# Forty columns of x a group on ScalarE from twenty packed words, and sixteen rows a group on the sync engine

## The chip, the cores and the metric

The kernel runs on one core of one Trainium2 chip. The metric is the device time of one launch in microseconds (us), the median of several runs. The engines named below are TensorE (PE, with PEld for its weight loads), VectorE (DVE), ScalarE (ACT), GpSimd (POOL) and the sync engine (SP); each runs its own list of instructions in order, and they meet through semaphores.

## The reference, cut to what matters

One layer of a graph network with attention over edges: 12500 nodes of 128 numbers, 212500 edges sorted by destination, 8 heads of 16 numbers.

```
Q, K, V = x @ WQ, x @ WK, x @ WV            # 12500 nodes, 8 heads of 16
Eh = edge_attr @ WE                         # 212500 edges
score = K[src] * Q[dst] / sqrt(16) * Eh
score = exp(clip(score.sum(-1), -5, 5))     # one number per edge and head
wV = segment_sum(V[src] * score, dst)
Z  = segment_sum(score, dst)
h  = x + wV / (Z + 1e-6)
y  = batchnorm over nodes(h) * gamma + beta
out = layernorm over features(x + y)
```

Everything is float32. The costly part is random access: each edge needs the K and V rows (256 numbers, 1 KB) of its source node.

## The kernel before, in words

The edges are cut into 1661 tiles of 128, in sorted order. A **group** is 8 tiles (the last has 5); there are 208 groups, numbered g from 0. The kernel first makes a table `kvd` in DRAM with the K and V row of every node, and keeps x, turned so that a node is a column of 128 numbers, in SBUF as `hx`. Then one loop over g (line 1004) does all edge work. In its iteration:

- DVE multiplies the gathered K rows of the group, which lie in a `slot`, by the edge projection and by the query in PSUM (`products`, L790: twice against `ps_e`, twice against `ps_q`), sums over a head (`scores`, L797), clips (L806); ACT takes the exponent (`clip_exp`, L807 and L808); DVE multiplies the V rows by it (`message`, L812).
- PE projects the next group's edge attributes (`eh_mm`, L765), spreads the queries to the edges (`qe_mm`, L774), and sums the messages by destination (`gather_sum`, L833).
- ACT takes the window of x for the queries (`q_window`, L719) and brings results out of PSUM (`q_out` L752, `sums_out` L838, `x_out` L875 and L876).

The K and V rows of a tile come into the slot in one of four ways. A tile is one of the 8 of its group, and only the last tile of a group (number 7) is ever fetched in another way than the first:

1. **A gather.** POOL issues one indirect DMA for the 128 rows of a tile (L290). Nine slots go round; when `message` of a group has been recorded, its slot is free and the gathers of a later group are queued (`load_kv`); `pace` ties each gather to a step of the iteration, so that they are spread over it.
2. **Columns on ACT** (`load_cols`, `fetch_cols`, L368 to L383). ACT loads node ids from `col_ids` into registers (L372) and copies, for each id, one column of `hx` into a tile `xc`, 128x1 an instruction (L383). In each group from 8 on it fetches COLS = 32: a load of 16 ids and 16 copies ahead of the exponent, a second load of 16 ids ahead of the exponent too, and 16 copies after it. When 128 columns are there, PE multiplies them by the K and V weights (`cols_mm`, L420) and ACT brings the 128 rows into the slot (`cols_out`, L425). The planner `col_plan` gives 49 groups whose last tile comes so.
3. **Rows on SP** (`fetch_rows`, L389 to L404). SP loads SP_ROWS = 8 ids a group from `row_ids` (L394) and issues one DMA of 1 KB for each, from `kvd` into a tile `byrow` (L401). When 128 rows are there, ACT copies the tile into the slot (`rows_out`, L411). `row_plan` gives 12 groups.
4. **Columns on DVE** (`fetch_v`, L364): 12 a group, 18 groups by `v_plan`.

So 49 + 12 + 18 = 79 groups need 7 gathers, not 8, and POOL issues 1518 gathers from `kvd`. Which group is served in which way follows from COLS, SP_ROWS and V_COLS alone; the ids of these tiles are put side by side on the host in that order.

SP's list also holds the loads of edge attributes (`load`, L700, 1 MB for two groups, ahead of the multiplication by two groups or more), the places of edges (`load_quad`, L588, once in four groups), and, about every ninth group, the write of 512 finished columns of h and the refill of their ring buffer (`keep_h`, L523 and L519). These wait for buffers that DVE, PE or ACT must have finished with.

An expression over registers, such as the address of a column from a node id, becomes one register instruction (FUSED_REGOPS in the trace) ahead of the copy that uses it.

Of the kernel before, what the change touches and what calls it, by code (L numbers as in the profile page):

```python
# [11 lines left out]
I32 = mybir.dt.int32  # L12
AF = mybir.ActivationFunctionType
OP = mybir.AluOpType
AX = mybir.AxisListType
ET = mybir.EngineType

P = 128
# [15 lines left out]
RING = 1024  # L34
MARGIN = 64
PAD = 2 * MARGIN + WN
COLS = 32
LOAD = 16
FIRST_COL = 8
COL_LAG = 3  # L40
SP_ROWS = 8
FIRST_ROW = 8
ROW_LAG = 2
NSEM = 6
# [31 lines left out]
def col_plan(sizes):  # L76
    full = sizes.count(U) // 2
    groups, end = [], P
    while FIRST_COL + -(-end // COLS) - 1 + COL_LAG < full:
        groups.append(max(NX, FIRST_COL + -(-end // COLS) - 1 + COL_LAG))  # L80
        end += P
    assert sorted(set(groups)) == groups
    return groups


def row_plan(sizes):
    full, used = sizes.count(U) // 2, set(col_plan(sizes))
    groups, end = [], P
    while True:
        g = FIRST_ROW + -(-end // SP_ROWS) + ROW_LAG  # L90
        while g in used:
            g += 1
        if g >= full:
            return groups
        used.add(g)
        groups.append(g)
        end += P


def v_plan(sizes):  # L100
    full, used = sizes.count(U) // 2, set(col_plan(sizes) + row_plan(sizes))
    tiles, at, end = [], [], P
    while True:
        m = FIRST_COL + -(-end // V_COLS)
        while (m - FIRST_COL) * COLS % P < COLS:
            m += 1
        g = m + COL_LAG - 1
        while g in used:
            g += 1
        if g >= full:  # L110
            return tiles, at
        used.add(g)
        tiles.append(g)
        at.append(m)
        end += P
# [7 lines left out]
def gnn_kernel(  # L123
# [19 lines left out]
    nc = tc.nc  # L143
    N, D = out.shape
# [10 lines left out]
    consts = ctx.enter_context(tc.tile_pool(name="consts", bufs=1))  # L155
# [53 lines left out]
    hx = consts.tile([P, N + P], F32, name="hx")  # L209
# [66 lines left out]
    def slot(i):  # L276
        return rows.tile([P, 2 * G * P], F32, name=f"slot{i}")

    first = slot(NSLOT).rearrange("p (h c d) -> p h c d", h=2, d=2 * P)
# [21 lines left out]
    def issue(n=0):  # L301
        while len(queued) > n:
            f, *a = queued.pop(0)
            f(*a)
# [11 lines left out]
    tot = len(col_tiles) * P  # L316
    assert -(-tot // (2 * COLS)) <= P and COLS == 2 * LOAD
    col_ids = consts.tile([P, 2 * COLS], I32, name="col_ids")
    row_tiles = row_plan(usizes)
    tot_rows = len(row_tiles) * P  # L320
    assert tot_rows % (2 * SP_ROWS) == 0 and row_tiles == sorted(row_tiles)
    v_tiles, v_at = v_plan(usizes)
# [4 lines left out]
    XV = {}  # L327
    row_ids = consts.tile([P, 2 * SP_ROWS], I32, name="row_ids")
    nc.vector.memset(row_ids, 0)
# [3 lines left out]
    XC = {}  # L333
# [3 lines left out]
    def load_ids(to, n, first, total):  # L337
        m, rest = divmod(total, n)
        for p, k, w in ((0, m, n), (m, 1, rest)):
            if w and k:  # L340
                nc.sync.dma_start(to[p:p + k, :w], bass.AP(
                    tensor=rsrc.tensor, offset=rsrc.offset + first + n * p, ap=[[n, k], [1, w]]))

    def load_col_ids():
        load_ids(col_ids, 2 * COLS, 0, tot)
        load_ids(row_ids, 2 * SP_ROWS, tot, tot_rows)
        load_ids(v_ids, 2 * V_COLS, tot + tot_rows, tot_v)
# [17 lines left out]

    OFFS = {}

    def load_cols(g, half):  # L368
        q = g - FIRST_COL
        if 0 <= q < -(-tot // COLS):  # L370
            at = q % 2 * COLS + half * LOAD
            _, offs = nc.values_load_multi_w_load_instructions(  # L372
                col_ids[q // 2:q // 2 + 1, at:at + LOAD], engines=(ET.Activation,), min_val=0, max_val=N - 1,
                skip_runtime_bounds_check_because="node ids")
            OFFS[g, half] = offs

    def fetch_cols(g, half):
        first = (g - FIRST_COL) * COLS + half * LOAD
        for r, off in zip(range(first, tot), OFFS.get((g, half), ())):
            k = col_tiles[r // P]  # L380
            if r % P == 0:
                XC[k] = late[0].tile([P, P], F32, name="xc", bufs=2)
            nc.scalar.activation(XC[k][:, r % P:r % P + 1], hx[:, ds(off, 1)], AF.Copy)  # L383

    def col_tile(g):
        q = (g - FIRST_COL) * COLS
# [2 lines left out]
    def fetch_rows(g):  # L389
        q = g - FIRST_ROW  # L390
        if not 0 <= q < tot_rows // SP_ROWS:
            return
        c = q % 2 * SP_ROWS
        _, offs = nc.values_load_multi_w_load_instructions(  # L394
            row_ids[q // 2:q // 2 + 1, c:c + SP_ROWS], engines=(ET.SP,), min_val=0,
            max_val=(N - 1) * 8 * P, skip_runtime_bounds_check_because="node ids")
        for r, off in enumerate(offs, q * SP_ROWS):
            k = r // P
            if r % P == 0:
                BY_ROW[k] = late[0].tile([P, 2 * P], F32, name="byrow", bufs=2)  # L400
            d = nc.sync.dma_start(BY_ROW[k][r % P:r % P + 1, :].bitcast(U8), kvb[ds(off, 8 * P)].unsqueeze(0))  # L401
            d.then_inc(rows_in[k % NSEM], 16)
            tc.no_tile_sem_insts.add(d.ins.name)
            tc.add_to_no_dep_group(f"rows{k}", d.ins)  # L404
# [78 lines left out]
    def within(f, g):  # L483
        return f(g) if 0 <= g < NG else None
# [100 lines left out]
    def load_quad(q):  # L585
        t = late[0].tile([P, RQ, U * P], U8, name="rbq", bufs=2)
        for h in (0, 1):
            nc.sync.dma_start(t[h * WN:(h + 1) * WN].rearrange("p a b -> p (a b)"), places(h, RQ * q, RQ))  # L588
        for k in range(RQ):
            RB[RQ * q + k] = t[:, k, :]  # L590
# [337 lines left out]
    for q in range(NQ):  # L928
# [13 lines left out]
        k = q - first_step  # L942
# [56 lines left out]
    def share(g):  # L999
        denom(g)  # L1000
        recip(g)
        attn(g)

    for g in range(NG - 2):
        within(load_rel, g + 3)
        if (g + 6) % RQ == 0 and (g + 6) // RQ in quads:
            load_quad((g + 6) // RQ)
        fetch_rows(g)
        if g % 2:
            load((g - 1) // 2 + 2)  # L1010
        within(products, g)
        within(scores, g)
        load_v(g)
        load_cols(g, 0)
        fetch_cols(g, 0)
        load_cols(g, 1)
        within(clip_exp, g)
        within(turned_onehot, g + 2)
        if g >= 2:
            share(g - 2)  # L1020
        late_x = g + 1 < nxg and g + 1 not in SLOT
        if late_x:
            turn_x(g + 1, 0, True)
            turn_x(g + 1, 4, True)
            project_main(g + 1)
        within(eh_mm, g + 1)
        within(qe_mm, g + 1)
        cols_mm(g)
        paced = g >= LATE + 4
        if not paced:  # L1030
            issue()
        else:
            issue(G)
            for step in (SENT[g - 1], PARTS[g][1], BY["eh", g + 1], PARTS[g][3], PARTS[g][4], BY["qe", g + 1]):
                pace(step)
        within(onehot, g + 1)
        if paced:
            pace(BY["one", g + 1])
        within(message, g)
        fetch_cols(g, 1)  # L1040
        within(q_window, g + 4)
        cols_out(g)
        rows_out(g)
        fetch_v(g)
        within(add_x, g - 3)
        within(q_mm, g + 3)
        within(gather_sum, g - 1)
        if paced:
            pace(BY["sum", g - 1])
        within(x_out, g - 3)  # L1050
        within(q_out, g + 3)
        within(sums_out, g - 1)
        if g == 2:
            load_last()
            nc.vector.tensor_scalar(row_ids, row_ids, 8 * P, None, op0=OP.mult)
        if g % (RUN // 2) == 2 and g > 2 and (g // (RUN // 2) + 1) * SEC < T:
            load_section(g // (RUN // 2) + 1)
        for i, r in enumerate(runs):
            if i and g == placed[i]:
                place(r)  # L1060
        within_checks(g)
        while free and todo and todo[0] in done and not pending:
            load_x()
        bn_parts(2 * g - 7, 2 * g - 5)
        if g == NG - 4:
            assert done >= set(range(NPRE))
            norm_first()
        if g == LATE - 1:
            tps.close()
            late.append(tps.enter_context(tc.tile_pool(name="late", bufs=1)))  # L1070
        if g == LATE - 2:
            free.append(NSLOT)
            load_kv()
    last = NG - 1
    g = last - 1
# [3 lines left out]
                           skip_runtime_bounds_check_because="a count")]  # L1079
# [332 lines left out]
```

## Time and profile before

| | |
|---|---|
| time, median of 3 runs | 2052.56 us (2050.99 to 2053.51) |
| the profiled execution | 2056.0 us, span of its instructions 2054.1 us |
| busy share of the span | PE 78%, PEld 63%, DVE 80%, ACT 51%, POOL 75% |
| mean granted TensorE clock | 0.874 |
| gathers from `kvd` on POOL | 1518, mean 952 ns |
| column copies on ACT | 6272, mean 190 ns |
| row DMAs on SP | 1536 |
| DMA queues' share of 16 engines | 33.2% (POOL's gathers), 24.2% (SP's) |

Busy time leaves out register, branch and semaphore instructions and the issue of DMAs, so SP has no busy share at all and ACT's does not hold its register loads. The idle time before an instruction is given with what ended it; "issue" there means that the engine waited for nothing that the profile shows. An engine that is idle in every step may still be the one that sets the pace, if its instructions follow each other at a fixed distance.

### The profile page before, as it was taken

To read this page: it belongs to the slowest core of one execution; us is meant where nothing else is said; L and a number is where in the kernel's file an instruction comes from. 1 tells how busy PE (TensorE), PEld (TensorE's weight loads), DVE (VectorE), ACT (ScalarE), POOL (GpSimd) and SP (SyncE) were. 2 spreads that over 40 slices of the span, in tenths; PEclk is the share of its full clock that TensorE was granted. 3 is DMA by queue.
4 is the path that set the end of the run, shared out by engine and by line. 5 is a ranking of instruction groups with operands and counts; after the bars stand their busy time and mean duration, and the time that the engine had idled before them with its cause. 6 is when DMAs were issued, how large, how long until landed. Compare 5 with 4: busy or idle time off the path is not lost.

```text
span 2054.1 us, 58951 instructions
## 1 busy us (share of the span) xinstructions
PE 1612.4 (78%) x12867; PEld 1300.0 (63%) x12867; DVE 1645.6 (80%) x5263; ACT 1046.3 (51%) x8290; POOL 1535.1 (75%) x1618
## 2 busy tenths in 40 slices
PE   7889888878777787777787877887877777777777
PEld 6777666666555665665566665666666666655666
DVE  4468999998887788788787887877877787877787
ACT  2245656664554555455455455454555555555436
POOL 7677777777777777777777777777777777777775
PEclk9899989998898888888888889888888898888899
DMA  7856655665555555555555556555555555555573
GB/s 262 294 174 186 205 184 174 200 203 168 172 184 176 173 184 168 175 183 168 181 182 178 170 170 190 179 162 186 184 159 187 183 158 185 165 178 184 170 245 128
DMA packets 130284, 377.69 MB, mean 184 GB/s; under 512 B 36112, under 2 KB 47547, under 8 KB 116091
## 3 DMA queue, kind: packets, MB, share of 16 engines
q0 software_dynamic: 74912, 203.26, 33.2%
q1 hardware_dynamic: 51816, 169.43, 24.2%
q14 instruction: 267, 2.18, 0.3%
q8 instruction: 103, 1.69, 0.3%
q10 hardware_dynamic: 3186, 1.13, 0.2%
HBM read 348.25 MB, written 25.44 MB: 182 GB/s over the span
## 4 chain that ended last, share of the span: by engine, by line
DVE 27%; DMA 25%; PE 20%; issue 19%; POOL 5%; ACT 2%; DVEq 2%; ACTq 0%; SPq 0%; POOLq 0%
DMA slot<-kvd,srcs 23%; DVE slot L790 9%; DVE s L797 8%; PE ps_q L774 5%; POOL slot L290 5%; PE ps_e L765 4%; PE ps_a L833 3%; DVE xv L364 2%; DVE ot L738 2%; PE ps_a L858 1%; DVEq L364 1%; DVE msg L812 1%; PE ps_e L900 1%; DVE s L806 1%; PE ps_q L900 1%
## 5 line engine op out<-in xcount | busy, mean ns | idle before, releaser
L290 POOL DMA_INDIRECT slot<-kvd,srcs x1518 | 1445.7, 952 | 467.0 <-issue 282.3
L383 ACT ACTIVATE xc<-hx 128x1 f32 x6272 | 647.0, 190 | 176.8 <-issue 142.6
L765 PE MATMUL ps_e<-w_e,ea 128*128 128x128 f32 x3322 | 496.7, 301 | 215.7 <-DVE slot L790 206.2
L765 PEld LDWEIGHTS ps_e<-w_e,ea 128*128 128x128 f32 x3322 | 431.6, 205 | 281.5 <-DVE slot L790 238.2
L774 PE MATMUL ps_q<-qs,ot 64*128 64x128 f32 x3322 | 374.3, 338 | 166.8 <-DVE slot L790 153.8
L790 DVE TENSOR_TENSOR slot<-slot,ps_e 128x512 f32<-128x512 f32 x410 | 273.2, 679 | 239.2 <-DMA slot<-kvd,srcs 202.0
L774 PEld LDWEIGHTS ps_q<-qs,ot 64*128 64x128 f32 x3322 | 303.5, 230 | 228.2 <-DVE slot L790 211.4
L833 PE MATMUL ps_a<-msg,oh 128*64 128x136 f32 x3322 | 316.5, 316 | 1.9 <-DVE msg L812 1.7
L807 ACT ACTIVATE ps_m<-s 128x64 f32<-128x64 f32 (+1 forms) x209 | 47.6, 228 | 500.6 <-DVE s L806 471.2
L797 DVE TENSOR_REDUCE s<-slot 128x64 f32<-128x1024 f32 (+1 forms) x208 | 249.9, 1202 | 19.4 <-DVE slot L790 0.9
L790 DVE TENSOR_TENSOR slot<-slot,ps_q 128x512 f32<-128x512 f32 x410 | 261.5, 678 | 1.0 <-PE ps_q L774 0.7
L833 PEld LDWEIGHTS ps_a<-msg,oh 128*64 128x64 f32 x3322 | 202.9, 150 | 88.4 <-issue 68.4
L812 DVE TENSOR_TENSOR msg<-slot,ps_m 128x1024 f32<-128x1024 f32 (+2 forms) x209 | 247.8, 1187 | 2.1 <-ACT ps_m L807 1.3
L876 ACT ACTIVATE ring<-ps_a 128x64 f32 x408 | 90.7, 222 | 155.1 <-PE ps_a L833 139.1
L364 DVE COPY xv<-hx 128x1 f32 x2304 | 155.8, 143 | 0.0
L731 DVE TENSOR_TENSOR oh<-ps_i,rel 128x512 f32<-128x512 f32 x208 | 141.7, 681 | 0.0
L858 PE MATMUL ps_a<-ident,at 128*128 128x128 f32 x408 | 112.5, 365 | 0.9 <-ACT os L838 0.9
L719 ACT ACTIVATE xw<-hx 128x64 f32 x416 | 82.4, 245 | 41.7 <-issue 23.6
L858 PEld LDWEIGHTS ps_a<-ident,at 128*128 128x128 f32 x408 | 81.6, 231 | 28.9 <-issue 5.6
L748 PE MATMUL ps_a<-w_q,xw 128*128 128x128 f32 x416 | 96.8, 321 | 0.4 <-ACT qs L752 0.4
L859 PE MATMUL ps_a<-xw,ident 128*128 128x128 f32 x408 | 95.8, 324 | 0.0
L738 DVE TENSOR_SCALAR ot<-rbq,wiota 128x512 f32<-128x512 uint8 x188 | 95.3, 507 | 0.0
(187 smaller groups left out, 1471.7 us busy)
## 6 DMA issues: line engine op xcount, KB each, us to landing
ea<-eaT SPq DMA_DIRECT2D x103, 1024.0 KB
byrow<-kvd SPq DMA_DIRECT2D x1536, 1.0 KB
slot<-kvd,srcs POOLq DMA_INDIRECT x1518
rbq<-relT SPq DMA_DIRECT2D x94, 128.0 KB
kvd<-slot SPq DMA_DIRECT2D x12, 512.0 KB
kvd<-t SPq DMA_DIRECT2D x12, 512.0 KB
ring<-xT SPq DMA_DIRECT2D x24, 256.0 KB
hT<-ring SPq DMA_DIRECT2D x23, 256.0 KB
```

What stands on the lines that cost most here:

```text
L290: return nc.gpsimd.indirect_dma_start(out=out, out_offset=None, in_=table, in_offset=bass.IndirectOffsetOnAxis(ap=part(SRC, e, 1), axis=0))
L364: nc.vector.tensor_copy(XV[k][:, r % P:r % P + 1], hx[:, ds(off, 1)])
L383: nc.scalar.activation(XC[k][:, r % P:r % P + 1], hx[:, ds(off, 1)], AF.Copy)
L731: by(("one", g), nc.vector.tensor_tensor(one, iota_ps[:, None, :WN].to_broadcast([P, k, WN]), r[:, :, None].to_broadcast([P, k, WN]), op=O ...
L738: by(("ot", g), nc.vector.tensor_scalar(OT[g], RB[g], wiota, None, op0=OP.is_equal))
L765: by(("eh", g), nc.tensor.matmul(t[:, j - a, :], EA[g][:, j, :], w_e, start=True, stop=True))
L774: by(("qe", g), nc.tensor.matmul(QE[g][h][:, j, :], OT[g][r, j * P:(j + 1) * P], QS[g][r], start=True, stop=True))
L790: step = nc.vector.tensor_tensor(kv, kv, of[g][i][:, :b - a, :], op=OP.mult)
L797: step = nc.vector.tensor_reduce(SS[g][:, a:b, :], KV[g](a, b, 0).rearrange("p t (h d) -> p t h d", d=DH), axis=AX.X, op=OP.add)
L812: step = nc.vector.tensor_tensor(MSG[g][:, a:b, :P].rearrange("p t (h d) -> p t h d", d=DH), KV[g](a, b, P).rearrange("p t (h d) -> p t h ...
L833: by(("sum", g), nc.tensor.matmul(AGG[g][h * WN:(h + 1) * WN], OH[g][h * n + j], MSG[g][:, h * n + j, :], start=(j == 0), stop=(j == k - 1)))
L858: nc.tensor.matmul(ps, AT[g], ident, start=True, stop=False)
```

## The change

COLS goes from 32 to 40 and LOAD from 16 to 20; SP_ROWS goes from 8 to 16. Once, in iteration 2, DVE packs the node ids two to a 32-bit word (`pack_ids`: the odd one shifted left by 16, or-ed with the even one; an id is below 12500). `load_cols` becomes one load of 20 words a group; the two ids of a word are `w % 65536` and `w >> 16`, register expressions in front of the copy that uses them. The 40 copies stand as 20 ahead of the exponent and 20 after `message`. The planners are as before and give 61 groups by columns on ACT, 24 by rows on SP and 18 by columns on DVE: 103 groups with 7 gathers, 1494 gathers in all.

```diff
-COLS = 32
-LOAD = 16
+COLS = 40
+LOAD = 20
...
-SP_ROWS = 8
+SP_ROWS = 16
...
+    col_pairs = consts.tile([P, COLS], I32, name="col_pairs")
+    assert N < 1 << 15 and LOAD % 2 == 0
...
-    def load_cols(g, half):
+    def pack_ids():
+        two = col_ids.rearrange("p (n c) -> p n c", c=2)
+        nc.vector.scalar_tensor_tensor(col_pairs, two[:, :, 1], 16, two[:, :, 0], op0=OP.logical_shift_left,
+                                       op1=OP.bitwise_or)
+
+    def load_cols(g):
         q = g - FIRST_COL
         if 0 <= q < -(-tot // COLS):
-            at = q % 2 * COLS + half * LOAD
-            _, offs = nc.values_load_multi_w_load_instructions(
-                col_ids[q // 2:q // 2 + 1, at:at + LOAD], engines=(ET.Activation,), min_val=0, max_val=N - 1,
-                skip_runtime_bounds_check_because="node ids")
-            OFFS[g, half] = offs
+            at = q % 2 * COLS // 2
+            _, words = nc.values_load_multi_w_load_instructions(
+                col_pairs[q // 2:q // 2 + 1, at:at + COLS // 2], engines=(ET.Activation,), min_val=0,
+                max_val=(N << 16) - 1, skip_runtime_bounds_check_because="node ids")
+            OFFS[g] = [e for w in words for e in (w % (1 << 16), w >> 16)]
+
+    def column(at):
+        return hx[:, ds(nc.s_assert_within(at, 0, N - 1, skip_runtime_bounds_check_because="node ids"), 1)]
 
     def fetch_cols(g, half):
         first = (g - FIRST_COL) * COLS + half * LOAD
-        for r, off in zip(range(first, tot), OFFS.get((g, half), ())):
+        for r, at in zip(range(first, tot), OFFS.get(g, ())[half * LOAD:half * LOAD + LOAD]):
...
-            nc.scalar.activation(XC[k][:, r % P:r % P + 1], hx[:, ds(off, 1)], AF.Copy)
+            nc.scalar.activation(XC[k][:, r % P:r % P + 1], column(at), AF.Copy)
...
-        load_cols(g, 0)
+        load_cols(g)
         fetch_cols(g, 0)
-        load_cols(g, 1)
...
         if g == 2:
             load_last()
             nc.vector.tensor_scalar(row_ids, row_ids, 8 * P, None, op0=OP.mult)
+            pack_ids()
```

The line numbers of the changed kernel are 2 higher around the id tiles and 10 higher after the functions above (ACT's column copy is L393, the row DMA L411, the exponent L817).

On POOL, the gathers of groups 14 to 21, one row a group, before:

```order
L290 DMA slot_1108<-kvd,srcs 128x256 x7
L290 DMA slot_1334<-kvd,srcs 128x256 x8
L290 DMA slot_1399<-kvd,srcs 128x256 x8
L290 DMA slot_1669<-kvd,srcs 128x256 x8
L290 DMA slot_1916<-kvd,srcs 128x256 x7
L290 DMA slot_2162<-kvd,srcs 128x256 x8
L290 DMA slot_2408<-kvd,srcs 128x256 x8
L290 DMA slot_2654<-kvd,srcs 128x256 x7
```

and in the changed kernel:

```order
L290 DMA slot_1111<-kvd,srcs 128x256 x7
L290 DMA slot_1337<-kvd,srcs 128x256 x8
L290 DMA slot_1402<-kvd,srcs 128x256 x8
L290 DMA slot_1675<-kvd,srcs 128x256 x7
L290 DMA slot_1928<-kvd,srcs 128x256 x7
L290 DMA slot_2181<-kvd,srcs 128x256 x8
L290 DMA slot_2435<-kvd,srcs 128x256 x7
L290 DMA slot_2687<-kvd,srcs 128x256 x7
```

Five of these eight groups have 7 gathers where three had; over the program it is 24 gathers fewer, and nothing else moves on POOL.

On ACT, the place around the exponent of one group in the middle of the loop (the ISA rows are the register instructions that make a column's address), before:

```order
L383 ISA
L383 ACTIVATE xc<-hx 128x1
L372 TENSOR_LOAD col_ids
L807 ACTIVATE ps_m<-s 128x64
L808 ACTIVATE msg<-s 128x8x8
L383 ISA
L383 ACTIVATE xc<-hx 128x1
```

and in the changed kernel:

```order
L393 ISA
L393 ACTIVATE xc<-hx 128x1
L817 ACTIVATE ps_m<-s 128x64
L818 ACTIVATE msg<-s 128x8x8
L393 ISA
L393 ACTIVATE xc<-hx 128x1
```

The load between the copies and the exponent is gone, and one load of 20 words stands ahead of the first copy; there is still one register instruction for each copy, which now holds three operations (remainder or quotient, multiply, add) where it held two (multiply, add).

On SP, two groups in the middle of the loop, before:

```order
L700 DMA ea<-eaT 128x2048
L588 DMA rbq<-relT 64x2048 x2
L394 TENSOR_LOAD row_ids
L401 DMA byrow<-kvd 1x1024 x8
L394 TENSOR_LOAD row_ids
L401 DMA byrow<-kvd 1x1024 x8
L700 DMA ea<-eaT 128x2048
```

and in the changed kernel:

```order
L710 DMA ea<-eaT 128x2048
L598 DMA rbq<-relT 64x2048 x2
L404 TENSOR_LOAD row_ids
L411 DMA byrow<-kvd 1x1024 x16
L404 TENSOR_LOAD row_ids
L411 DMA byrow<-kvd 1x1024 x16
L710 DMA ea<-eaT 128x2048
```

Sixteen row DMAs stand where eight did, so a load of edge attributes is issued behind 32 row DMAs since the one before it, not behind 16.

## The prediction

> **What bounds the kernel now.** I read the table of engines first: DVE 80%, PE 78%, POOL 75%, ACT 51%, none full. So the question goes to the waits, and there I began with the engine that never rests, POOL, by its timeline: here the first two gathers from `kvd` and the last two, with start, duration, and in brackets the idle time before.
>
> ```profile
> 90.95 0.94 POOL L290 DMA_INDIRECT slot<-kvd,srcs  x1 [4.69 <-issue]
> 92.20 0.95 POOL L290 DMA_INDIRECT slot<-kvd,srcs  x1 [0.30 <-issue]
> ...
> 1996.76 0.95 POOL L290 DMA_INDIRECT slot<-kvd,srcs  x1 [0.30 <-issue]
> 1998.01 0.95 POOL L290 DMA_INDIRECT slot<-kvd,srcs  x1 [0.30 <-issue]
> ```
>
> 1518 gathers lie between 90.95 and 1998.01, so they follow each other every 1907.06 / 1517 = 1.257 us, and the two ends show the plain spacing: 0.95 busy and 0.30 between, 1.25. Nearly nothing is left for waiting. The waits of POOL, DVE and ACT from 820 to 1990 us (total, times, longest) and the number of groups DVE did there say the same:
>
> ```profile
> POOL slot L290 <- issue: 164.5, 540, 0.3
> ...
> DVE slot L790 <- DMA slot<-kvd,srcs: 152.9, 91, 5.4
> ...
> L797 DVE TENSOR_REDUCE s<-slot 128x64 f32<-128x1024 f32 x123 | 150.0, 1220 | 11.3
> ...
> ACT ps_m L807 <- DVE s L806: 293.3, 106, 7.1
> ACT ring L876 <- PE ps_a L833: 84.6, 46, 3.5
> ACT ring L875 <- PE ps_a L833: 25.3, 14, 2.8
> ```
>
> POOL's longest wait is the 0.3 us that stands before every gather; no step, slot or transfer holds it up. DVE waits for gathers to land. A group takes 1170 / 123 = 9.51 us, of which DVE waits 152.9 / 123 = 1.24 for gathers; left alone it would need about 8.27. POOL needs 1518 / 200 x 1.257 = 9.54 a group (groups 8 to 207). So **the issue of gathers on POOL** sets the loop's end, DVE is second with 1.2 us of room, and ACT waits (293.3 + 84.6 + 25.3) / 123 = 3.28 us a group for others.
>
> **The change, part by part.**
>
> *Gathers removed.* 1518 become 1494: 24 x 1.257 = **30.2 us** off a chain without gaps. POOL then needs 1494 / 200 x 1.257 = 9.39 us a group, still 1.1 above DVE's own 8.27, so all of it should arrive at the end. After the last gather nothing is changed, and the 56 us from there to the span's end stay. All 24 saved gathers belong to groups before the last few, so none is saved too late.
>
> *ACT: loads, copies, register work.* Rows of single lines (shortest, median, longest ns), and two runs of 16 copies:
>
> ```profile
> L383 ACTq FUSED_REGOPS  x6272: 37/37/37, 169.7 to 1974.5; - x196
> L875 ACTq FUSED_REGOPS  x83: 51/51/57, 250.8 to 1999.7; - x83
> L372 ACTq TENSOR_LOAD <-col_ids x392: 1007/1048/1461, 168.6 to 1969.4; - x196
> L866 ACTq TENSOR_LOAD <-ring_i x104: 306/312/488, 125.4 to 2008.0; - x104
> ...
> 1003.24 1.67 ACT L383 ACTIVATE xc<-hx 128x1 f32 x16 [0.62 <-issue]
> ...
> 1008.57 0.23 ACT L807 ACTIVATE ps_m<-s 128x64 f32<-128x64 f32 x1 [3.67 <-DVE s L806]
> 1008.73 0.24 ACT L808 ACTIVATE msg<-s 128x64 f32<-128x64 f32 x1
> 1008.88 1.57 ACT L383 ACTIVATE xc<-hx 128x1 f32 x16
> ```
>
> A load of 16 words takes 1.048, one of 4 words 0.312: 0.061 a word, so 20 words take 1.048 + 4 x 0.061 = 1.29. Two loads (2.10) become that one: -0.81 a group. Sixteen copies take 1.67 or 1.57, so one every (1.67 - 0.19) / 15 = 0.099 or 0.092, say 0.097; eight more are +0.78. Together -0.03: the packing pays for the columns. What is left is the added register operation of all 40 copies. The remainder and the quotient are in no row. Below, it costs nothing, if it falls into the spacing of the copies. The nearest row is L875, which adds one more term to an address than L383 does: 51 against 37 ns, 14 an operation. Above, I take the dearest work per register that the trace has, 61 ns a loaded word. A group then grows by 0, 0.56 or 2.45 us; I take 0.56, since that is the same instruction with one operation more. Even 2.45 lies within ACT's 3.28 (3.16 at the new pace). Ahead of the exponent stand one load and 20 copies, 1.29 + 20 x 0.111 = 3.5 us, where two loads and 16 copies took 3.65: the exponent is no later, and it waited 3.67 for DVE in the row above. Behind `message` the copies grow from 16 x 0.097 to 20 x 0.111, by 0.67; queued behind them are the window of x, `cols_out`, `rows_out`, `x_out` and `sums_out`. Those who wait for these are DVE and PE, and DVE's 1.24 us covers it; without that cover it would be 0.67 x 200 = 134 us. The 12 more `cols_out` and 12 more `rows_out` (0.38 and 0.41 each) are 10 us in all on ACT, 0.05 a group.
>
> *SP: sixteen rows.* SP's queue over eight groups, and its load:
>
> ```profile
> 999.67 1.10 SPq L588 DMA_DIRECT2D rbq<-relT  x2
> 1001.91 5.94 SPq L401 DMA_DIRECT2D byrow<-kvd  x16
> 1007.97 0.36 SPq L700 DMA_DIRECT2D ea<-eaT  x1
> 1009.22 6.72 SPq L401 DMA_DIRECT2D byrow<-kvd  x16
> 1025.02 0.36 SPq L700 DMA_DIRECT2D ea<-eaT  x1
> 1038.73 1.10 SPq L588 DMA_DIRECT2D rbq<-relT  x2
> 1040.98 5.96 SPq L401 DMA_DIRECT2D byrow<-kvd  x16
> 1047.03 0.36 SPq L700 DMA_DIRECT2D ea<-eaT  x1
> 1062.62 0.35 SPq L523 DMA_DIRECT2D hT<-ring  x1
> 1064.98 0.33 SPq L519 DMA_DIRECT2D ring<-xT  x1
> 1066.22 6.12 SPq L401 DMA_DIRECT2D byrow<-kvd  x16
> 1072.45 0.36 SPq L700 DMA_DIRECT2D ea<-eaT  x1
> 1075.23 1.09 SPq L588 DMA_DIRECT2D rbq<-relT  x2
> 1077.45 2.55 SPq L401 DMA_DIRECT2D byrow<-kvd  x8
> ...
> L394 SPq TENSOR_LOAD <-row_ids x192: 712/799/1001, 164.7 to 1909.7; - x192
> L401 SPq DMA_DIRECT2D byrow<-kvd x1536: 224/228/512, 166.6 to 1912.9; - x192
> ```
>
> Eight rows take 2.55, one every (2.55 - 0.23) / 7 = 0.33. Eight more are 2.65, and eight more words to load 8 x 0.061 = 0.49: +3.1 us a group, 25 us over these eight groups. SP's three long idle stretches there (1015.94 to 1025.02, 1025.38 to 1038.73, 1047.39 to 1062.62) are 9.1 + 13.4 + 15.2 = 37.7. So SP has room, but uses two thirds of it. A group's SP work becomes 16 x 0.33 + 1.29 + 0.18 (half of a load of edge attributes) + 0.28 (a quarter of `rbq`) + 0.3 (ring) = 7.3 us of 9.39.
>
> What gets late is what stands behind the rows. The edge attributes of two groups (1.05 MB) are asked for as soon as their buffer is free, two groups or 19 us ahead of use; behind four more groups' worth of eight rows they go out some 6 to 12 us later than now. The transfer itself I estimate from the window's rate:
>
> ```profile
> 820.00:1990.00 1170.00, 906.17 (x7193) 723.12 (x7193) 939.32 (x3078) 596.54 (x4949) 886.01 (x933) 0.85 0.57 180
> ```
>
> 1.05 MB at 180 GB/s (the last number) is 5.8 us, so 19 - 5.8 = 13 us are spare: enough, but no longer ample. The rows themselves have two groups (ROW_LAG) to land.
>
> [...]
>
> *PE and DVE.* Twelve more `cols_mm` fall on PE, which waits for DVE anyway; `pack_ids` is one small instruction of DVE in iteration 2, before the loop is short of anything. Both nothing.
>
> **Sum.** The profiled execution took 2056.0 (span 2054.1): 2056.0 - 30.2 = 2025.8. It lies 3.4 above the median of the runs, so for the median **2022.5**.
>
> **Rivals.**
>
> *A. ACT's remainders and quotients make it slower.* A remainder and a quotient are worked out for each of 20 words, in some 196 groups. ACT's room is 3.16 us a group; 40 of them fill it at 79 ns each, and at 83 ns the kernel is as slow as before (0.15 us x 200 groups = the 30 us won). At 100 ns it is 0.84 x 196 = 165 us over the forecast: about **2188**. For it: no row has such an operation, and it stands twice in every group, with the exponent behind one half. Against: one more operation costs 14 ns in L875, and a multiply is already among the two in L383.
> [...]
>
> *B. The edge attributes come late.* If SP's lateness eats the 13 us and PE waits w us for each load, DVE's pace becomes 8.27 + w / 2. That is nothing until w = 2.2; at w = 2.4 a group takes 9.47, 0.08 x 200 = 16 us more: about **2039**. For it: SP falls behind whenever a ring refill has held it for 15 us. Against: the idle stretches above let it catch up.
>
> *C. SP cannot keep up.* Its work passes 9.39 us when a row costs (9.39 - 2.05) / 16 = 0.46. At 0.51, the longest single issue in the row of L401, it is 10.2 a group, 0.8 x 192 = 155 us: about **2178**. Against: the median is 0.228 for the issue and 0.33 for the spacing.
>
> *D. The gain is lost in the start.* Early on DVE is behind POOL, and saved gathers could make POOL wait for slots. Then only the later ones count, and the time nears **2050**. Against: POOL's 0.30 us before a gather stays the same from 92 us on.
>
> **How the numbers follow.** The forecast, POOL's chain shorter by 24 gathers, has 0.80; its own range is 2017 to 2030 (the whole 30 us and a few us of noise, or a quarter of it lost at stalls). B has 0.06, A 0.07, C 0.03, D 0.04. The range 2017 to 2042 takes in the forecast and most of B. A measurement tells 0.2%, about 4 us, from no change: faster 0.80 + 0.05 from B = 0.85; same 0.05 from D and the end of B; slower 0.10 from A and C.
>
> **What would show it.** Right: 1494 gathers still every 1.25 to 1.26 us with 0.30 before them, the last near 1968; DVE's waits for gathers a little shorter (1.1 us a group); ACT's register instruction near 51 ns and its wait for DVE before the exponent near 2 us. Wrong: gaps before gathers (D), register instructions of 80 ns or more and DVE waiting for the exponent (A), PE waiting for `ea` (B), SP's queue without idle stretches (C).

## The result

The changed kernel takes 2021.17 us (median of 4 runs, 2019.15 to 2024.75) beside 2051.77 for the kernel before: 30.6 us less, ratio 0.985 with a 95% interval of 0.9836 to 0.9865. The prediction said 2022.5, between 2017 and 2042. The profiled execution took 2024.75 us, with a span of 2022.9. Nine of the twelve experiments below ran on two other chips, on which the kernel before itself takes 2620 or 2650 us, so each is compared with the kernel before on its own chip only, and what those two chips can tell is said apart.

### The profile after

POOL's timeline in the changed kernel: the first two gathers from `kvd` and the last two.

```profile
90.00 0.94 POOL L290 DMA_INDIRECT slot<-kvd,srcs  x1 [4.80 <-issue]
91.25 0.95 POOL L290 DMA_INDIRECT slot<-kvd,srcs  x1 [0.30 <-issue]
...
1964.80 0.95 POOL L290 DMA_INDIRECT slot<-kvd,srcs  x1 [0.30 <-issue]
1966.05 0.95 POOL L290 DMA_INDIRECT slot<-kvd,srcs  x1 [0.30 <-DVE slot L800]
```

1494 gathers in 1876.05 us are 1876.05 / 1493 = 1.2566 us each: the same spacing, 24 fewer. The last one starts 31.96 us earlier than before (1998.01 to 1966.05). The chain began 0.95 earlier, 24 x 1.257 = 30.2 are the gathers, and the last 0.8 are the mean spacing, which is shorter by a little over 0.0005 us at each of 1493 gathers. What follows the last gather took 56.1 us and now takes 56.9, so the span is 31.2 shorter.

The waits of DVE, PE and ACT (total, times, longest) from 820 to 1960 us, and the 122 groups that DVE did there:

```profile
DVE slot L800 <- DMA slot<-kvd,srcs: 125.0, 67, 5.1
DVE stats L889 <- ACT ring L886: 23.7, 14, 3.1
DVE msg L822 <- ACT ps_m L817: 9.0, 18, 1.0
...
L807 DVE TENSOR_REDUCE s<-slot 128x64 f32<-128x1024 f32 x122 | 148.8, 1220 | 10.8
...
PE ps_e L775 <- ACT slot L435: 28.6, 13, 3.3
PE ps_e L775 <- DMA ea<-eaT: 0.6, 1, 0.6
...
ACT ps_m L817 <- DVE s L816: 58.2, 38, 5.0
ACT ring L886 <- PE ps_a L843: 21.8, 25, 2.3
ACT ring L885 <- PE ps_a L843: 4.9, 7, 1.2
```

DVE still waits 125.0 / 122 = 1.02 us a group for gathers (1.24 before), so POOL is still the bound. The edge attributes come in time. What changed most is ACT: its waits, (58.2 + 21.8 + 4.9) / 122 = 0.70 us a group, were 3.28 in the same three rows (what of that was room is worked out below), and DVE and PE have begun to wait for it. Two lines and the timeline of one group say why; the columns of the first are the shortest, median and longest time in ns.

```profile
L393 ACTq FUSED_REGOPS  x7808: 73/77/100, 168.1 to 1940.1; - x196
L379 ACTq TENSOR_LOAD <-col_pairs x196: 1238/1296/2062, 166.7 to 1937.6; - x196
...
1001.86 2.83 ACT L393 ACTIVATE xc<-hx 128x1 f32 x20 [0.91 <-issue]
1004.60 0.21 ACT L817 ACTIVATE ps_m<-s 128x64 f32<-128x64 f32 x1
1004.74 0.24 ACT L818 ACTIVATE msg<-s 128x64 f32<-128x64 f32 x1
1004.89 1.78 ACT L393 ACTIVATE xc<-hx 128x1 f32 x14
```

The load of 20 words takes 1.296, as reckoned (1.29). The register instruction takes 77 ns, not 51: a remainder or a quotient of a word took 40 ns more here than the instruction without it (37, L383 before), where an added term took 14 (51, L885). Twenty copies take 2.83, one every (2.83 - 0.19) / 19 = 0.139 us; before it was 0.097. In this group ACT comes out of its 20 copies just as the exponent is due, without a wait.

SP's queue, the first seven of its entries from 999 to 1080 us, and its two lines:

```profile
999.78 0.36 SPq L710 DMA_DIRECT2D ea<-eaT  x1
1001.51 11.99 SPq L411 DMA_DIRECT2D byrow<-kvd  x32
1013.62 0.36 SPq L710 DMA_DIRECT2D ea<-eaT  x1
1023.35 1.11 SPq L598 DMA_DIRECT2D rbq<-relT  x2
1026.05 11.93 SPq L411 DMA_DIRECT2D byrow<-kvd  x32
1038.07 0.36 SPq L710 DMA_DIRECT2D ea<-eaT  x1
1044.26 0.35 SPq L533 DMA_DIRECT2D hT<-ring  x1
...
L404 SPq TENSOR_LOAD <-row_ids x192: 1158/1258/1489, 162.8 to 1887.5; - x192
L411 SPq DMA_DIRECT2D byrow<-kvd x3072: 224/228/415, 164.7 to 1893.7; - x192
```

Thirty-two rows and the load between them take 12 us, so a row still goes out every 0.33 us and a load of 16 ids takes 1.26. The long idle stretches shrank to 1013.98 to 1023.35 and 1038.43 to 1044.26, 15 us where 38 were; the prediction's 37.7 less 25 left 13. From there to 1080 us SP is never idle for longer than 3.1 us.

### The profile page after: what moved, and what is told of

Read it like the earlier page. It is cut to its first block, busy times and chain, and to the rows that moved or that the text cites. A ratio compares the mean times of both kernels' runs of the same rounds, so it can differ in the third digit from the quotient of the medians.

```text
span 2022.9 us, 65020 instructions
## 1 busy us (share of the span) xinstructions
PE 1609.2 (80%) x12891; PEld 1308.4 (65%) x12891; DVE 1648.2 (81%) x5264; ACT 1467.7 (73%) x9850; POOL 1511.8 (75%) x1594
## 4 chain that ended last, share of the span: by engine, by line
issue 22%; DMA 19%; DVE 19%; PE 16%; ACT 15%; POOL 4%; ACTq 2%; DVEq 1%; SPq 1%; POOLq 0%
DMA slot<-kvd,srcs 17%; ACT xc L393 10%; DVE slot L800 7%; DVE s L807 5%; POOL slot L290 4%; PE ps_q L784 4%; PE ps_e L775 3%; PE ps_a L843 2%; DVE xv L366 2%; ACT ring L886 2%; DVE ot L748 1%; PE ps_e L487 1%; PE ps_q L910 1%; PE ps_e L910 1%; DVEq L366 1%
## 5 line engine op out<-in xcount | busy, mean ns | idle before, releaser
L290 POOL DMA_INDIRECT slot<-kvd,srcs x1494 | 1421.9, 952 | 459.9 <-issue 283.4
L393 ACT ACTIVATE xc<-hx 128x1 f32 x7808 | 1073.3, 201 | 248.2 <-issue 215.5
L775 PE MATMUL ps_e<-w_e,ea 128*128 128x128 f32 x3322 | 524.7, 313 | 269.7 <-DVE slot L800 209.1
L775 PEld LDWEIGHTS ps_e<-w_e,ea 128*128 128x128 f32 x3322 | 458.3, 216 | 335.3 <-DVE slot L800 243.5
L784 PE MATMUL ps_q<-qs,ot 64*128 64x128 f32 x3322 | 358.0, 340 | 84.6 <-DVE slot L800 74.2
L784 PEld LDWEIGHTS ps_q<-qs,ot 64*128 64x128 f32 x3322 | 294.6, 234 | 138.2 <-DVE slot L800 121.0
L800 DVE TENSOR_TENSOR slot<-slot,ps_e 128x512 f32<-128x512 f32 x410 | 268.1, 679 | 141.5 <-DMA slot<-kvd,srcs 125.0
L843 PE MATMUL ps_a<-msg,oh 128*64 128x136 f32 x3322 | 305.1, 307 | 1.7 <-DVE msg L822 1.7
L843 PEld LDWEIGHTS ps_a<-msg,oh 128*64 128x64 f32 x3322 | 194.5, 145 | 83.9 <-issue 61.6
L868 PE MATMUL ps_a<-ident,at 128*128 128x128 f32 x408 | 107.0, 350 | 1.2 <-ACT os L848 1.2
L817 ACT ACTIVATE ps_m<-s 128x64 f32<-128x64 f32 (+1 forms) x209 | 45.0, 215 | 76.6 <-DVE s L816 75.2
L758 PE MATMUL ps_a<-w_q,xw 128*128 128x128 f32 x416 | 91.7, 307 | 0.4 <-ACT qs L762 0.4
```

Of the source, the lines that this page charges most:

```text
L290: return nc.gpsimd.indirect_dma_start(out=out, out_offset=None, in_=table, in_offset=bass.IndirectOffsetOnAxis(ap=part(SRC, e, 1), axis=0))
L393: nc.scalar.activation(XC[k][:, r % P:r % P + 1], column(at), AF.Copy)
L775: by(("eh", g), nc.tensor.matmul(t[:, j - a, :], EA[g][:, j, :], w_e, start=True, stop=True))
L784: by(("qe", g), nc.tensor.matmul(QE[g][h][:, j, :], OT[g][r, j * P:(j + 1) * P], QS[g][r], start=True, stop=True))
L800: step = nc.vector.tensor_tensor(kv, kv, of[g][i][:, :b - a, :], op=OP.mult)
L843: by(("sum", g), nc.tensor.matmul(AGG[g][h * WN:(h + 1) * WN], OH[g][h * n + j], MSG[g][:, h * n + j, :], start=(j == 0), stop=(j == k - 1)))
```

## Experiments

### Where the kernel before takes its 2052 to 2054 us

The theory to test was that the time follows the number of gathers on POOL and nothing else that the change does; its rivals, that a part of the gain comes from ACT's single load, or that only the packing makes 40 columns possible.

**The gathers alone.** The kernel before, with the gather of the last tile left out in 24 more groups. So that the slot holds numbers, one plain load of 128 KB on SP fills that tile with the table's first 128 rows: these tiles hold the K and V of the wrong nodes, and all else is computed.

```diff
+    left_out = [g for g in range(17, full - 1) if g not in apart][::4][:24]
...
-            for j in range(sizes[g] - (g in apart)):
+            for j in range(sizes[g] - (g in apart or g in left_out)):
...
+        if g + 4 in left_out:
+            nc.sync.dma_start(KV[g + 4](G - 1, G, 0, 2 * P)[:, 0, :], kvd[:P, :])
```

> The kernel before with 24 gathers taken away and nothing put on ACT or on rows: for 24 more groups (17 to 203) the last tile is filled by one plain 128 KB load on SP with the first 128 rows of the table, four groups ahead, in place of the gather. These 24 tiles thus hold the rows of the wrong nodes; everything else is computed. POOL issues 1494 gathers as in the changed kernel. Theory, where the kernel before takes its 2052 us: 24 x 1.257 = 30 us, ratio 0.985, the changed kernel's time without its ACT and SP work. Rival (part of the gain came from ACT's loads): 0.99 or more. Where the kernel before takes 2620 us or more (instructions of ACT, PE and SP stall there): theory A, a gather is worth 1.25 us there too, ratio 0.9885, and the changed kernel would be at 2678 - 30 = 2649, slower than before by its added instructions; theory B, gathers are hidden there, ratio 1.000 and the changed kernel as slow as with its gathers put back.

Measured: 2022.39 beside 2052.61, ratio 0.9851 (0.9835 to 0.9868). That is the whole gain of the change, with 32 columns and 8 rows as before. The line of the gathers over the run, the last gather, and a wait of ACT and one of DVE from 820 to 1960:

```profile
L290 POOL DMA_INDIRECT slot<-kvd,srcs x1494 | 1420.9, 951 | 459.9 <-issue 279.8 <-DVE slot L792 46.9 <-DMA slot<-kvd,srcs 31.7
...
1964.29 0.95 POOL L290 DMA_INDIRECT slot<-kvd,srcs  x1 [0.30 <-DVE slot L792]
...
ACT ps_m L809 <- DVE s L808: 284.9, 103, 6.5
...
DVE slot L792 <- DMA slot<-kvd,srcs: 139.7, 86, 4.8
```

ACT waits here as long as in the kernel before (284.9; it was 293.3 in a window 30 us longer), and the last gather comes within 2 us of the changed kernel's. So, to within the 3 us or so that these intervals leave open, ACT's and SP's new work adds nothing to the time and takes nothing from it: the gathers that it replaces are the gain.

**The change again, and without its packing.** Two kernels side by side on one chip: the changed kernel, and the kernel before with only three numbers changed, so that 40 ids come in two loads of 20 plain words.

```diff
-COLS = 32
-LOAD = 16
+COLS = 40
+LOAD = 20
...
-SP_ROWS = 8
+SP_ROWS = 16
```

> The changed kernel itself, beside the kernel before on one chip. Where the kernel before takes its 2052 us: 2021, ratio 0.985, as measured. Where it takes some 2620 to 2650 us, as in the five runs so far, ACT, PE and SP show waits of 0.7 us and multiples of it in the middle of batches that wait for nothing. There theory A (every gather still costs 1.25 us, and the added instructions of ACT and SP cost what the two halves alone showed, 17 + 15 and 12 + 15 us) gives +59 - 30 = +29, ratio 1.011; theory B (POOL is no longer the bound, so gathers are hidden) gives the same as with 24 gathers put back, ratio 1.021 to 1.024.

> The change without its packing: 40 columns a group and 16 rows, but the ids of the columns come in two loads of 20 plain words, the second ahead of the exponent as before. 1494 gathers as in the changed kernel. ACT's group costs 2 x 1.29 + 40 x 0.097 = 6.5 us in place of 1.29 + 40 x 0.139 = 6.9. Theory (the number of gathers sets the time while ACT has room): the same as the changed kernel within 4 us, 2021, ratio 0.985, with a longer wait of ACT for DVE before the exponent. Rival (the packing is what makes 40 columns possible): slower than the changed kernel by 10 us or more. Where instructions stall (the kernel before at 2620 or more), one more load a group should cost some 0.7 us a group at most.

Measured beside 2054.24: the changed kernel 2026.22, ratio 0.9865 (0.9848 to 0.9881); two loads of plain ids 2024.28, ratio 0.9853 (0.9836 to 0.9869). The same, and the rival falls: nothing in 40 columns needs the packing. The version without it (register instruction, load, then ACT's waits for DVE before the exponent, the last of them the changed kernel's, then both kernels' busy times from 820 to 1960, the changed one last; behind the window's length come the busy times of PE, PEld, DVE, ACT and POOL):

```profile
L383 ACTq FUSED_REGOPS  x7808: 37/37/37, 168.0 to 1939.2; - x196
L372 ACTq TENSOR_LOAD <-col_ids x391: 1242/1292/2052, 166.7 to 1937.0; - x196
...
ACT ps_m L807 <- DVE s L806: 143.0, 66, 4.8
ACT ps_m L807 <- DVE rz L845: 27.3, 23, 1.2
ACT ps_m L807 <- DVE oh L731: 22.5, 19, 1.2
...
ACT ps_m L817 <- DVE s L816: 58.6, 47, 5.8
...
820.00:1960.00 1140.00, 886.34 (x7157) 708.77 (x7153) 930.30 (x3041) 684.52 (x5829) 863.40 (x908) 0.86 0.57 183
...
820.00:1960.00 1140.00, 891.41 (x7181) 714.77 (x7179) 932.91 (x3046) 849.50 (x5847) 863.15 (x909) 0.86 0.57 183
```

Packing saves half of the loaded words, 61 / 2 = 31 ns an id at the 61 ns a word of the loads before, and costs 40 ns an id for taking it out again. ACT's busy time, 685 us in place of 850, and its longer waits make the plain version look much lighter than it is. A load is not counted as busy, and the second load of 1.29 us a group is 158 us in this window, nearly all of the 165 between the two. It also stands right ahead of the exponent: by the starts and ends of the loads in the trace, 130.8 of the 211.8 us that ACT is idle before its exponents pass while a load runs. What is left, 0.66 us a group, is little more than the 0.48 of the changed kernel, where no load falls into that wait. The plain version leaves ACT a few tenths of a microsecond a group more, at the same time to within what these runs tell apart.

### Where the kernel before takes 2620 or 2650 us

On two other chips ACT, PE and SP stood still in the middle of batches, for nothing that the records show. Parts of ACT's and PE's timelines of one of these kernels (16 rows, 32 columns) at the same moment, and the lines of the register instructions of ACT and DVE and of SP's row DMAs:

```profile
1514.09 0.56 ACT L383 ACTIVATE xc<-hx 128x1 f32 x5
1515.03 0.20 ACT L383 ACTIVATE xc<-hx 128x1 f32 x1 [0.39 <-issue]
1515.77 0.20 ACT L383 ACTIVATE xc<-hx 128x1 f32 x1 [0.53 <-issue]
1517.15 0.20 ACT L383 ACTIVATE xc<-hx 128x1 f32 x1 [1.18 <-issue]
1517.89 0.20 ACT L383 ACTIVATE xc<-hx 128x1 f32 x1 [0.54 <-issue]
...
1515.70 0.28 PE L830 MATMUL ps_a<-msg,oh 128*1 128x136 f32 x1 [0.92 <-issue]
1517.14 0.28 PE L833 MATMUL ps_a<-msg,oh 128*64 128x136 f32 x1 [1.16 <-issue]
1518.58 0.47 PE L833 MATMUL ps_a<-msg,oh 128*64 128x136 f32 x3 [1.17 <-issue]
...
L383 ACTq FUSED_REGOPS  x6272: 3/37/1422, 249.0 to 2582.9; - x196
L364 DVEq FUSED_REGOPS  x2304: 46/46/46, 252.0 to 2548.5; - x192
L401 SPq DMA_DIRECT2D byrow<-kvd x3072: 3/224/1444, 244.1 to 2551.7; - x192
```

ACT goes on in steps of about 0.72 us or twice that, PE in steps of 1.44, and the issue of a row on SP, 512 ns at most in the kernel before, takes up to 1444; the register instruction of DVE never takes more than its 46 ns. And POOL no longer goes without a break. This is the gathers' line of the kernel with the packing alone, 1518 gathers:

```profile
L290 POOL DMA_INDIRECT slot<-kvd,srcs x1518 | 1437.1, 947 | 998.4 <-remote 373.1 <-issue 290.2 <-PE ps_e L775 99.6
```

The idle time before gathers is 998.4 / 1518 = 0.66 us, not 0.30. So these chips cannot test the theory as it stands; they show what the change's parts cost where POOL's chain has breaks. The edits: the columns' half (the change with SP_ROWS = 8), the rows' half (the kernel before with SP_ROWS = 16), the packing alone (the change with COLS = 32, LOAD = 16 and SP_ROWS = 8), and the change with 24 gathers put back into a tile that nothing reads:

```diff
+    spare = consts.tile([P, 2 * P], F32, name="spare")
...
+            if g in row_tiles:
+                queued.append((gather, spare, kvd, starts[g] + sizes[g] - 1))
```

> The columns' half of the change alone: 40 columns a group from packed words, still 8 rows on SP. 61 + 12 + 18 groups are served otherwise, so 1506 gathers. Theory (only the number of gathers sets the time, 1.257 us each): 12 x 1.257 = 15.1 us below the kernel before, about 2037, and 15 above the changed kernel. Rival (the gain came from ACT's single load, or from SP's rows): all of the 30 us, 2021, or none of it, 2052. POOL's spacing stays 1.25 to 1.26.

> The rows' half alone: SP fetches 16 rows, ACT fetches 32 columns with two loads of 16 ids as before. 49 + 24 + 18 groups, 1506 gathers. Theory: 15.1 us below the kernel before, about 2037. Rival (SP's lateness costs DVE or PE something): above 2037. ACT should wait for DVE before the exponent as long as in the kernel before (293 us from 820 to 1990 us), since its work is the same.

> The packing alone: 32 columns from one load of 16 packed words, 8 rows; 1518 gathers as before. Theory: no change, 2052 within 4 us, although ACT does other work: one load of 1.05 us in place of two (-1.05 a group) and 32 copies at 0.139 in place of 0.097 us (+1.34), so ACT waits some 0.3 us a group less. Rival (the load saved is the gain): faster by more than 5 us.

> The changed kernel with 24 gathers put back: for each of the 24 groups whose last tile comes by rows, POOL gathers that tile too, into a spare tile that nothing reads. All of the change's work on ACT and SP stays; POOL issues 1518 gathers. Theory: all of the gain goes, 2021 + 24 x 1.257 = 2051, as the kernel before. Rival (the gain came from ACT or SP): stays near 2021.

The gathers put back and the columns' half were tried again on the second chip:

> The changed kernel with 24 gathers put back into a spare tile (for each group whose last tile comes by rows), 1518 in all; ACT and SP do the whole of the change's work. Theory (only the number of gathers sets the time): all of the gain goes, ratio 1.000 to the kernel before, POOL's gathers 1.25 to 1.26 us apart. Rival (the gain came from ACT's single load or elsewhere): ratio near 0.985. Should the kernel before take some 2650 us again, as in the four runs before this one, then its instructions stall and the ratio says nothing on the theory; PE and ACT would show waits of 0.5 to 1.2 us for nothing (issue) in the middle of a batch.

> The changed kernel with 24 gathers put back into a spare tile, 1518 in all; ACT and SP do all of the change's work. Theory (the number of gathers alone sets the time): the whole gain goes, 2054, ratio 1.000 within 0.002. Rival (part of the gain is ACT's single load or less waiting elsewhere): ratio clearly under 1, down to 0.986.

> The columns' half alone: 40 packed columns, 8 rows on SP, 1506 gathers. Theory: half of the gain, 12 x 1.257 = 15 us, ratio 0.9927. Rival (the rows bring it, the columns' unpacking eats their own gain): ratio 0.998 or more.

Two further kernels were also measured there only: the change with two more remainders on every other column, and a version with 48 columns on ACT from two loads of 24 plain ids, 16 rows on SP and 16 columns on DVE.

```diff
-            OFFS[g] = [e for w in words for e in (w % (1 << 16), w >> 16)]
+            OFFS[g] = [e for w in words for e in (((w % (1 << 16)) % ((1 << 14) + 1)) % (1 << 14), w >> 16)]
```

```diff
-COLS = 32
-LOAD = 16
+COLS = 48
+LOAD = 24
...
-SP_ROWS = 8
+SP_ROWS = 16
...
-V_COLS = 12
+V_COLS = 16
```

> The changed kernel with two more remainders for the even one of the two ids of a word (by 16385 and by 16384, which leave an id as it is): a remainder costs 40 ns by the changed kernel's trace (77 against 37), so these 20 columns a group take about 157 ns of register work and are 0.22 apart, the other 20 stay at 0.139. ACT gets 20 x 0.08 = 1.6 us more a group, 80 ns a column above the kernel before where the prediction put the threshold at 79. What ACT has left in the changed kernel: it waits (58.2 + 21.8 + 4.9) / 122 = 0.70 us a group for DVE and PE, and DVE waits 125 / 122 = 1.02 for gathers. Theory now (ACT and DVE wait for each other, so only the smaller leftovers count and ACT takes the bound): a group takes 9.39 + 1.6 - 0.70 = 10.3, at most, 0.9 x 196 = 176 us slower, about 2200; if DVE's wait for gathers may be used up as well, 0 to 30 us slower. The prediction's threshold: no slower than the kernel before, 2022 to 2052.

> A version that goes further along the same way without packing: 48 columns a group on ACT with two loads of 24 plain ids, 16 rows on SP, and 16 columns in place of 12 on DVE. 73 + 24 + 24 groups, 1476 gathers, 18 fewer than the changed kernel. Theory (POOL is still the bound): 18 x 1.257 = 22.6 us below the changed kernel, about 2001, ratio 0.975. ACT's group: 2 x 1.54 + 48 x 0.097 = 7.7 us of loads and columns, 0.9 more than in the changed kernel; DVE's: 4 more columns and 4 more words, 4 x 0.067 + 4 x 0.06 = 0.5. Rival (ACT's 0.70 us a group are gone, and it takes the bound): 0 to 40 us above the changed kernel, 2021 to 2060.

Measured, each beside the kernel before on its chip:

| kernel | gathers | this, us | before, us | ratio (95%) |
|---|---|---|---|---|
| columns alone | 1506 | 2667.08 | 2650.11 | 1.0065 (1.0048 to 1.0082) |
| rows alone | 1506 | 2661.85 | 2650.11 | 1.0048 (1.0031 to 1.0065) |
| packing alone | 1518 | 2649.54 | 2650.11 | 0.9995 (0.9983 to 1.0008) |
| 24 gathers back | 1518 | 2706.12 | 2650.11 | 1.0212 (1.0195 to 1.0229) |
| 24 gathers back, second chip | 1518 | 2680.87 | 2619.70 | 1.0236 (1.0219 to 1.0253) |
| 24 gathers back, second chip | 1518 | 2678.35 | 2619.67 | 1.0221 (1.0204 to 1.0238) |
| columns alone, second chip | 1506 | 2638.80 | 2619.67 | 1.0068 (1.0051 to 1.0085) |
| dearer unpacking, second chip | 1494 | 2707.88 | 2619.67 | 1.0322 (1.0301 to 1.0343) |
| more columns, second chip | 1476 | 2785.66 | 2619.67 | 1.0622 (1.0604 to 1.0641) |

Here the expectations of the theory missed, all but one: the halves do not win 15 us, they lose 17 and 12 (and 19 on the second chip). The packing alone changes nothing, as expected, in spite of its dearer copies. Where a rival's words fit (the rows above 2037, the columns at 0.998 or more), it was written for a chip on which POOL goes without a break, and these runs don't show it for that chip. Each of the two halves takes work from POOL and gives it to ACT or SP, and on these chips that is a loss.

Whether a gather is worth anything there is not settled. The two halves together have 24 gathers fewer and lose 17 + 12 = 29; all of the change's work with the gathers put back loses 56. If losses add up, the difference of 27 is 24 gathers at 1.1 us, and the whole change would lose about 29 us there (2650 to 2679). But that they add up was not shown, and the changed kernel itself was not run on these chips. The dearer unpacking (88 us over) and the version with more columns (166 over) were meant to find the point from which ACT decides on a chip where POOL is the bound; they did not get to one, so that point, and whether more columns would win there, stay open. The dearer unpacking does give the price of a remainder once more: of its register instructions, those with two more remainders mostly took 157 ns and the others mostly 76 (86 is the median of all 7808), so 40 for each remainder.

## Why the prediction was right, and where its steps were off

*The bound and its price.* Right, and shown: the gathers kept their spacing (1.2566 after 1.2571), the end moved by their number, and taking 24 gathers away, with no new work for ACT and only 24 plain loads for SP in their place, gave the same 0.985 as the change. The opposite test, the changed kernel with 24 gathers put back, ran on the two other chips alone, so that side is not shown. The forecast of the profiled execution, 2025.8, was 1.1 us high.

*ACT's register operation.* The step that priced it at 14 ns, "since that is the same instruction with one operation more", was mis-sized: 40 ns measured, inside the bounds of 0 and 61. A group of ACT grew by 40 x 0.042 = 1.7 us by it, not by 0.56.

*ACT's room.* This step was wrong too. 3.28 us of waiting a group was read as room. But in the kernel before a part of the idle time before the exponent was the second load of ids, which isn't counted as busy. In the group that the prediction shows, ACT's copies end at 1004.91 and the exponent starts at 1008.57. The load between them, and two waits of PE and DVE for ACT in the kernel before (820 to 1990 us):

```profile
L372 ACTq TENSOR_LOAD <-col_ids x1: 1033/1033/1033, 1004.7 to 1004.7; - x1
...
PE ps_e L765 <- ACT slot L425: 4.0, 5, 1.4
...
DVE msg L812 <- ACT ps_m L807: 0.6, 2, 0.4
```

From 1004.7 the load ran to 1005.7, so 0.8 of the 3.67 us were not a wait for DVE. Over the window 103.9 of the 313.4 us that ACT is idle before its exponents pass while a load runs, 0.85 us a group. The true room was about 3.28 - 0.85 = 2.4, or 2.3 at the new pace, which makes the threshold of rival A 2.3 / 40 = 58 ns, not 79. With 42 ns the change used up some three quarters of it; 2.3 - 1.7 = 0.6 agrees with the 0.70 that were measured. The sentence "Even 2.45 lies within ACT's 3.28" was therefore wrong: 61 ns an operation, which the prediction allowed for, would have passed the threshold by this reckoning. That the operation cost 40 and not 61 was luck as far as the working goes.

The step "the exponent is no later" failed with it: 1.30 + 20 x 0.139 = 4.1 us stand ahead of the exponent, where 3.5 were reckoned and 3.65 stood before, and DVE's message now waits for ACT 18 times in the window, where it waited twice. ACT's wait for DVE before the exponent, forecast near 2 us a group, came out as 58.2 / 122 = 0.48.

*What covered it.* DVE's room, by all that the runs show, as the prediction said it would have to. With 24 gathers taken away and no new work on ACT, DVE waits 139.7 / 122 = 1.15 us a group for gathers; in the changed kernel it waits 1.02 for them, and its waits for ACT have grown to (23.7 + 9.0) / 122 = 0.27. PE's wait for `cols_out` rose from 4.0 to 28.6 us, behind the same cover.

*SP.* Right in each term: 0.33 us a row, 1.26 for the load, idle stretches that shrink and do not vanish, the edge attributes in time (rival B would have shown as PE waiting for `ea`, which it did once, for 0.6 us). Rival C would have needed 0.46 a row. The 5.8 us for a transfer of edge attributes came from the rate of all transfers together and was not measured; that they come in time is what PE's row shows.

*Rival D* did not happen: no two gathers of the changed kernel, from the first to the last, start more than 1.52 us apart. *Rival A* did not happen on the chip of the result, but by a smaller margin than was thought; whether it decides at 58 ns was not measured. The sign that the prediction gave for it, a register instruction of 80 ns or more, took the price of the operation for that of the whole instruction: 79 ns more than 37 would have been 116. The 77 ns measured lay just under a sign that was set too low.

*What the prediction did not see* is that the sign of such a step can hang on the chip: on two other chips, where instructions stalled for 0.72 or 1.44 us, the halves of this change, tried alone, cost time (the columns 17 and 19 us, the rows, tried on one of the two, 12).

## What to carry to other kernels

Where one engine issues the same instruction at a fixed spacing from the loop's start to its end, the time of the loop is count times spacing, however moderate its busy share looks (here 1518 gathers at 1.2571 us and 1494 at 1.2566, with POOL 75% busy both times); take the work off that engine, and read each receiver's room from its own waits. Subtract from those waits the register loads and DMA issues that the profile does not count as busy: the wait before the exponent was a third shorter than it looked (103.9 of 313.4 us). And before packing values to save loads, price the taking apart: 31 ns saved an id, 40 ns spent.

## What the runs showed of the hardware that was not expected

- A register remainder by 65536 took 40 ns on ACT (77 against 37 ns for the instruction with one operation fewer), three times an added term (14: 51 against 37). The shift by 16 cost the same to within 2 ns (medians 78 for the remainder, 76 for the shift, 77 for both together).
- The same program ran 28 and 29% longer on two other chips (2052, 2620 and 2650 us), with gathers and column copies that lasted as long (a gather 947 ns in the mean with the packing alone there, a copy 191 in the median with the rows alone; 952 and 191 on the first chip). ACT, PE and SP stopped there between instructions, in steps of about 0.72 us or twice that, while POOL's gathers and DVE's register instructions (46 ns on both) kept their durations; the mean granted TensorE clock was 0.78 and 0.79 there and 0.87 on the first chip. What stopped them, and how much of the 28 and 29% is due to it, is not known from these runs.
